# A two-layer Perceiver kernel: the separate context row's product made ahead on GpSimd, one addition for each bank of averages, full-width transposes of the last rows

## The chip, the cores and the metric

The kernel runs on one core of a Trainium2 chip. The metric is the device time of one execution, in microseconds, as the median of several runs.

The core's engines work at once, each through its own instructions in order: TensorE (PE, with its weight loads as PEld), VectorE (DVE), ScalarE (ACT), GpSimd (POOL) and SyncE (SP), which here only issues DMA transfers. They wait for each other by semaphores. Matrix products land in PSUM, which has banks of 512 fp32 numbers for each of 128 partitions; everything else lies in SBUF.

## What is computed

There are 16 batches of 64 latent tokens of width 128 (x), and for each batch a context of 1601 rows. Two layers follow each other; each adds to x a cross-attention over the context, a scan (a state-space recurrence) and a feed-forward part (in layer 0 a small attention with a mixture of experts, in layer 1 a linear block with values rounded to a coarse grid). All is fp32. The part that the change touches most is the cross-attention, cut to its core:

```python
xn, ln_lat = layer_norm(x, g1, b1), layer_norm(latents, g2, b2)
q = ln_lat @ Wq
k, v = split(concatenate([xn, ln_lat], axis=1) @ Wkv)      # 1601 + 64 rows, 16 heads of 64
weight = softmax(where(mask, einsum('bhld,bhnd->bhln', q, k) * scale, neg))
out = einsum('bhln,bhnd->bhld', weight, v) @ Wout
```

The scan of layer 0 runs 16 states over 64 tokens: h = exp(A dt) h + dt u B_t, y = sum over the states of h C_t.

## The kernel before

**Attention.** Weights are folded so that queries meet the normalised context rows directly, and averages of context rows are projected afterwards. A *group* is one layer, one batch and half of the heads: 64 groups in order, each with 512 columns (8 heads of 64 queries). A group has 13 steps (NT), one for each 128 keys: rows 0 to 1535 in 12 chunks, and a last chunk of 64 context rows (1536 to 1599) with the 64 latents below them. Row 1600, the *row apart*, does not fit; it is treated by itself.

At each step n the function step() writes, in this order: scores() of the newest group (L706, a 128x512 product into one of three PSUM banks "s"; L714 or L716, the running maximum R on VectorE; L719 or L721, the eviction to st on ScalarE); average() of the group begun LAG = 23 steps earlier (L820, two banks "av", one for each pair of query blocks, with a 129th column that sums the weights); gather() at that group's end; then the steps of self.plan for the group between: partial, joint, handed, everywhere, own_max, apart_weight at fixed step numbers counted from the group's end, which find each column's maximum, and weigh(), which subtracts it (L807) and takes the exponential (L808). fp32 products appear twice in the profile, as two passes.

**The row apart.** For each group apart_weight() makes ee, its weight for each query: df is subtracted on VectorE (L786) from the group's own maxima m4, which came by DMA (L779), and ScalarE takes the exponential (L787). xeb is the normalised row with a 1 behind it, broadcast to all partitions by a DMA 14 steps into the batch (L1595). gather() leaves PSUM and adds the row at once: for each of the two banks, two instructions on VectorE (L829) make aq = xeb * ee + av. Then denominator() takes reciprocals (L868) and scales aq on GpSimd (L869), turn() transposes, and output() projects. The very last group goes through finish() instead.

**Context.** In layer 0, context() normalises a batch's rows (L666, L675), writes them to DRAM for layer 1, transposes them four chunks at a time on TensorE (L685) and evicts the result twice on ScalarE (L688, for layer 0 and for layer 1); the last chunk goes as a 64-row transpose. GpSimd then scales the rows (L624), and a DMA puts the latents into the last chunk's lower half (L626). The first batch takes a path of its own (first_context), with its own 64-row transpose at L574.

**Everything else** lies beside it. The stages scan0 and moe (layer 0, four rounds) and scan1 and ffn (layer 1, five rounds) are generators; run() advances them with a budget for each step, so that they fill the engines beside the attention of later batches. The scan of scan0 has for each state s two exponentials (L977), a product db on GpSimd (L978), the scan itself on VectorE (L989), a product with C (L994) and a sum on GpSimd (L995). B and C rows come broadcast by DMA as bb, two states at a time (L974).

A scheduler orders the instructions of each engine; the contexts behind() keep new work from going further ahead than a given earlier score step on TensorE, VectorE and ScalarE. Buffers are rotating tiles: a tile of the same tag waits until the earlier one's readers are done.

Of the kernel before, what the change touches and what calls it, by code (L numbers as in the profile page):

```python
# [32 lines left out]
F32 = mybir.dt.float32  # L33
# [4 lines left out]
ALU = mybir.AluOpType  # L38
# [4 lines left out]
P = 128  # L43
NB, L, D = 16, 64, 128
# [3 lines left out]
G = 12  # L48
REM = 64
# [18 lines left out]
NS = 16  # L68
# [10 lines left out]
TG = CG * P  # L79
# [4 lines left out]
class Kernel:  # L84
# [543 lines left out]
    def context(self, lay, b):  # L628

        nc = self.nc  # L630
        w1, b1 = self.vecs_of(lay)[:2]
        kv, kvT = self.kv_of[lay, b]
        n = G + 1
        if (lay, b) == (0, 1):

            mv = self.sm([P, n, 2], "fmv", bufs=2)
            rstd, off = (self.sm([P, n], f"c{x}") for x in ("rstd", "off"))
            for k in range(n):
                bs = self.sm([P, 6], "fbs")
                nc.vector.bn_stats(bs, kv[:, k, :D])  # L640
                nc.vector.bn_aggr(mv[:, k, :], bs)
                if k % 2:
                    yield 1.0
            nc.vector.tensor_scalar_add(rstd, mv[:, :, 1], EPS)
            self.rsqrt(rstd, rstd, n)
            nc.gpsimd.tensor_tensor(off, mv[:, :, 0], rstd, ALU.mult)
            nc.gpsimd.tensor_scalar(off, off, -1.0, None, ALU.mult)
            for k in range(8, n):
                nc.gpsimd.tensor_scalar(kv[:, k, :D], kv[:, k, :D], mv[:, k, 0:1], rstd[:, k:k + 1], ALU.subtract, ALU.mult)
            yield HOP3  # L650
            for k in range(8):
                nc.scalar.activation(kv[:, k, :D], kv[:, k, :D], AF.Identity, scale=rstd[:, k:k + 1], bias=off[:, k:k + 1])
                if k % 2:
                    yield 1.0
        elif lay == 0:
            nc.gpsimd.memset(kv[64:P, G, :D], 0.0)
            nmean, rstd, v, off = (self.sm([P, n], f"c{x}") for x in ("mean", "rstd", "var", "off"))
            for lo, hi in ((0, 7), (7, n)):
                nc.vector.tensor_reduce(nmean[:, lo:hi], kv[:, lo:hi, :D], AX.X, ALU.add)
                if lo == 0:  # L660
                    yield 1.0
            nc.vector.tensor_scalar_mul(nmean, nmean, -1.0 / D)
            yield 0.2
            for k in range(n):
                scr = self.at.tile([P, D], F32, tag="cscr", name=f"scr{b}_{k}", bufs=1)
                nc.scalar.activation(scr, kv[:, k, :D], AF.Square, bias=nmean[:, k:k + 1], accum_out=v[:, k:k + 1])  # L666
                if k in (3, 6, 9):
                    yield 0.0
            yield HOP1
            nc.vector.tensor_scalar(v, v, 1.0 / D, 1e-5, ALU.mult, ALU.add)  # L670
            self.rsqrt(rstd, v, n)
            nc.gpsimd.tensor_tensor(off, nmean, rstd, ALU.mult)  # L672
            yield HOP5
            for k in range(n):
                nc.scalar.activation(kv[:, k, :D], kv[:, k, :D], AF.Identity, scale=rstd[:, k:k + 1], bias=off[:, k:k + 1])  # L675
                if k in (3, 6, 9):
                    yield 0.0
        if lay == 0:
            nc.sync.dma_start(out=self.xh[b], in_=kv[:, :, :D])
            yield HOP  # L680
            for g in range(G // 4 + 1):
                w, m = (512, P) if g < G // 4 else (REM, REM)
                t = self.tp(f"kt{b}_{g}")
                for k in range(4 * g, min(4 * g + 4, n)):
                    nc.tensor.transpose(t[:, (k - 4 * g) * P:(k - 4 * g) * P + m], kv[:m, k, :D], self.ident[:m, :m])  # L685
                raw = self.at.tile([P, 512], F32, tag="kts", name=f"kts{b}_{g}", bufs=1)
                for to, by in ((kvT[:, g * 512:g * 512 + w], w1), (raw[:, :w], YG1)):
                    nc.scalar.activation(to, t[:, :w], AF.Copy, scale=self.vcol[:, by:by + 1])  # L688
                nc.sync.dma_start(out=self.xhT[b][:, g * 512:g * 512 + w], in_=raw[:, :w])
                yield HOP3  # L690
        yield from self.with_latents(lay, b)
# [89 lines left out]
    def apart_weight(self, g):  # L781
# [5 lines left out]
        nc.scalar.activation(ee, df, AF.Exp)  # L787
        grp["ee"] = ee

    def spread(self, v, name):  # L790

        t = self.tp(name)
        for k in range(4):
            self.nc.tensor.transpose(t[:, k * P:(k + 1) * P], v[:, k:k + 1].to_broadcast([P, P]), self.ident)  # L794
        return t
# [26 lines left out]
    def gather(self, g, j):  # L822

        nc, grp = self.nc, self.groups[g]
        if j == 0:
            grp["aq"] = self.at.tile([P, 4, D + 1], F32, tag="aq", name=f"aq{g}", bufs=2)
        xeb, av = self.xeb_of[grp["key"][:2]], grp.pop(("av", j))
        for k in range(2):
            nc.vector.scalar_tensor_tensor(grp["aq"][:, 2 * j + k, :], xeb, grp["ee"][:, 2 * j + k:2 * j + k + 1], av[:, k, :], ALU.mult, ALU.add)  # L829
        if j:  # L830
            for k in ("st", "R", "mb"):
                grp.pop(k)
# [66 lines left out]
    def scan0(self, gr):  # L899
        nc, tc, a = self.nc, self.tc, self.a  # L900
        X = self.X[:, gr * CG:(gr + 1) * CG, :]
        with tc.tile_pool(name="sc1", bufs=1) as one, ExitStack() as later:
            t1 = lambda shape, name: one.tile(shape, F32, tag=name, name=f"sc_{name}")
# [4 lines left out]
            two = lambda name: a[name].rearrange("(k p) n -> p k n", p=P)  # L908
# [16 lines left out]
            both = [P, 2, TG]  # L925
# [7 lines left out]
            g = self.tp("g")  # L933
            for k in range(2):
                nc.tensor.matmul(g[:, k * TG:(k + 1) * TG], W_gate[:, k * P:(k + 1) * P], xT, start=True, stop=True)
            th = t1(both, "y")
# [11 lines left out]
            t = self.tp("bc")  # L948
# [3 lines left out]
            bcd = self.dram.tile([2, NS, TG], F32, tag=f"bcd{gr}", name=f"bcd{gr}")  # L952
            nc.sync.dma_start(out=bcd.rearrange("j s t -> (j s) t"), in_=bcT)
            first.close()
            work = later.enter_context(tc.tile_pool(name="sc2", bufs=2))
# [5 lines left out]
            u = t1(both, "u")  # L961
# [4 lines left out]
            y = t1(both, "y")  # L966
            yield 1.2

            def ahead(s):
                nonlocal bb  # L970
                if s % 2 == 0:
                    bb = work.tile([P, 2, 2, TG], F32, tag="bb", name=f"bb{s}")
                    for j in range(2):
                        nc.sync.dma_start(out=bb[:, j], in_=bcd[j, s:s + 2, :].partition_broadcast(P))  # L974
                da, db = (work.tile(both, F32, tag=n, name=f"{n}{s}") for n in ("da", "db"))
                for k in range(2):
                    nc.scalar.activation(da[:, k, :], dt[:, k, :], AF.Exp, scale=na[:, k, s:s + 1])  # L977
                nc.gpsimd.tensor_tensor(db, u, self.row(bb[:, 0, s % 2, :], both), ALU.mult)  # L978
                return da, db, self.row(bb[:, 1, s % 2, :], both)

            bb = None
            made = ahead(0)
            yield HOP
            for s in range(NS):
                da, db, cc = made
# [237 lines left out]
    def scan1(self, c0, CG):  # L1223
        nc, tc, a = self.nc, self.tc, self.a
        X = self.X[:, c0:c0 + CG, :]
        TG, BG = CG * P, 2 * CG
        NH, HD = 4, 64
        last = c0 + CG == C and CG == 1
        with tc.tile_pool(name="sd1", bufs=1) as one, tc.tile_pool(name="sd2", bufs=CG) as work:
            t1 = lambda shape, name: one.tile(shape, F32, tag=name, name="sd_" + name)  # L1230
            ld = lambda name, shape, src=None: self.load(name, shape, a[name] if src is None else src, one)
            two = lambda name: a[name].rearrange("(k p) n -> p k n", p=P)
# [19 lines left out]
            xc, th = t1([P, 2, TG], "xc"), t1([P, 2, TG], "th")  # L1252
# [11 lines left out]
            else:  # L1264
                t = self.tp("xz")
# [19 lines left out]
            t = self.tp("sdt")  # L1285
# [3 lines left out]
            shape = [P, CG, NH]  # L1289
            dt, adt = t1(shape, "dt"), t1(shape, "adt")  # L1290
            e, w, v, ln = (t1(shape, n) for n in ("spe", "spw", "spv", "spl"))
# [7 lines left out]
            t = self.tp("sz")  # L1299
# [23 lines left out]
                        nc.tensor.matmul(t[:, hh * TG:(hh + 1) * TG], m[:, k, hh * P:(hh + 1) * P], xc[:, k, :], start=(k == 0), stop=(k == 1))  # L1323
                nc.scalar.copy(dst.rearrange("p h t -> p (h t)"), t[:, :2 * TG])

            bT, cT = t1([P, 2, TG], "bT"), t1([P, 2, TG], "cT")
            bc(bT, BwT)
            yield 0.4
            yield HOP1
# [5 lines left out]
            both = [slice(b * L, (b + 1) * L) for b in range(2)]  # L1335
            af = [work.tile(full, F32, tag="af", name=f"af{c}") for c in range(CG)]
            for c in range(CG):
                x = nc.vector.tensor_tensor(af[c], self.row(self.after, full), self.bc(adt[:, c, :], full), ALU.mult)
# [6 lines left out]
            t = self.tp("sx")  # L1345
# [13 lines left out]
            for c in range(CG):  # L1359
                gs = [self.tp(f"gr{c}{i}") for i in range(2)]  # L1360
                for k in range(2):
                    for i in range(2):
                        part = slice(i * HD, (i + 1) * HD)
# [16 lines left out]
            for dst, i in ((zb, 2), (z, 0)):  # L1380
                for k in range(2):
                    x = nc.scalar.activation(dst[:, k, :], z[:, k, :], AF.Copy, scale=self.ycol[:, i + k:i + k + 1])
# [19 lines left out]
            t = self.tp("syt")  # L1402
# [6 lines left out]
            t = t[:, :2 * TG]  # L1409
# [118 lines left out]
    def run(self, out):  # L1528
# [2 lines left out]
        self.groups = [{"key": (lay, b, half)} for lay in range(2) for b in range(NB) for half in range(2)]  # L1531
        ng = len(self.groups)
        self.plan = (
            ((0, self.partial), (2, self.joint), (3, self.handed), (5, self.everywhere), (7, self.own_max), (11, self.apart_weight)),
            ((1, self.maximum), (3, self.spread_max)),
        )
        per_layer = NB * 2 * NT
# [1 line left out]
        done = lambda lay, b: start(lay, b) + LAG + 10  # L1539
# [44 lines left out]
        while n < (ng + 1) * NT + LAG + 8 or between:  # L1584
            for lay in range(2):
                for b in range(NB):
# [6 lines left out]
                    if n == start(lay, b) + 14:  # L1593
                        xeb = self.xeb_of[lay, b] = self.at.tile([P, D + 1], F32, tag="xeb", name=f"xeb{lay}_{b}", bufs=2)
                        self.nc.sync.dma_start(out=xeb, in_=self.xed[lay][b].partition_broadcast(P))  # L1595
            while prep and prep[0][0] <= n:
                key, _, g = prep.pop(0)
# [191 lines left out]
```

## Time and profile before

| what | value |
|---|---|
| time, median of 3 runs | 1936.54 us (1932.92 to 1939.88) |
| the profiled execution's own time | 1938.11 us |
| its span, first to last instruction | 1936.4 us, TensorE's granted clock 0.996 |
| TensorE matmul busy | 1883.0 us, 97% (11738 instructions) |
| VectorE busy | 1633.4 us, 84% (3186) |
| ScalarE busy | 1357.9 us, 70% (2635) |
| GpSimd busy | 511.8 us, 26% (584) |
| score matmuls L706 | 862.8 us, 1664 passes |
| average matmuls L820 | 884.6 us, 6656 passes |
| gather L829 on VectorE | 76.7 us, 252 instructions |
| scaling L869 on GpSimd | 71.7 us, 63 instructions |
| DMA | 112.64 MB, mean 58 GB/s |

A row of the profile names line, engine and operation, output and inputs with their shapes, then the count; behind the bar stand the busy time and the mean length of one, and then the time that the engine sat idle just before and what ended that idle time. Shares of busy time are averages over stages that have different limits; a matmul's end is modelled, so that consecutive passes overlap in the rows. A wait row says who waited, for which line on which engine, the sum in us, the number of times and the longest.

### The profile page before, as it was taken

The numbers are of one execution on the slowest core, as the hardware profiler recorded it, in microseconds if no ns is written. First come the engines' busy times: TensorE is split into PE (matmuls) and PEld (weight loads), VectorE is DVE, ScalarE is ACT, GpSimd is POOL, SyncE is SP. The second block draws the span as 40 slices with busy tenths as digits, with TensorE's granted clock in tenths as the row PEclk, the third lists the DMA queues.
The fourth block names the chain that finished last, engine by engine and source line by source line (L and its number), as shares of the span: only waits on it lengthen the run. The fifth ranks groups of instructions, "written<-read, shape, count | busy, mean of one in ns | idle before, by whom it ended". The sixth has DMA issues, their size and how long they took to land. (4 is left out here: it accounts for less than half of the span.)

```text
span 1936.4 us, 32717 instructions
## 1 busy us (share of the span) xinstructions
PE 1883.0 (97%) x11738; PEld 1426.3 (74%) x11738; DVE 1633.4 (84%) x3186; ACT 1357.9 (70%) x2635; POOL 511.8 (26%) x584
## 2 busy tenths in 40 slices
PE   9999999998999999999999999999999999999998
PEld 5777777676777767777667787767778777776786
DVE  7987777998878998886998978999787998877984
ACT  5888887897869888776665757767566565765651
POOL 5122122543214453121443203453101121102000
PEclk9999999999999999999999999999999999999999
DMA  6121112321123131232232102222120211201100
GB/s 194 36 58 55 55 55 77 86 64 45 54 82 94 57 82 49 69 95 68 73 79 59 40 25 75 71 71 55 42 58 21 60 38 38 59 2 38 25 2 23
DMA packets 192268, 112.64 MB, mean 58 GB/s; under 512 B 56030, under 2 KB 174570, under 8 KB 192106
## 3 DMA queue, kind: packets, MB, share of 16 engines
q1 hardware_dynamic: 187278, 109.77, 20.6%
q8 instruction: 93, 1.52, 0.3%
q10 hardware_dynamic: 4828, 0.78, 0.2%
q14 instruction: 69, 0.57, 0.1%
HBM read 81.41 MB, written 27.54 MB: 56 GB/s over the span
## 5 line engine op out<-in xcount | busy, mean ns | idle before, releaser
L820 PEld LDWEIGHTS av<-kv,st 128*128 128x128 f32 x6656 | 870.2, 192 | 365.6 <-issue 346.3
L820 PE MATMUL av<-kv,st 128*128 128x129 f32 x6656 | 884.6, 276 | 2.2 <-DVE aq L829 2.1
L706 PE MATMUL s<-qT,kvT 128*128 128x512 f32 x1664 | 862.8, 601 | 15.7 <-ACT st L721 10.5
L808 ACT ACTIVATE st<-st 128x1024 f32<-128x1024 f32 (+1 forms) x448 | 444.4, 997 | 130.2 <-DVE st L807 124.2
L807 DVE TENSOR_TENSOR st<-st,mb 128x1024 f32<-128x1024 f32 (+1 forms) x448 | 504.2, 1130 | 2.0 <-PE mb L794 1.5
L719 ACT ACTIVATE st<-s,mcol 128x512 f32<-128x512 f32 x416 | 282.7, 683 | 219.4 <-DVE R L714 197.5
L721 ACT COPY st<-s 128x512 f32<-128x512 f32 x416 | 239.9, 582 | 108.1 <-DVE R L716 100.2
L714 DVE SCALAR_TENSOR_TENSOR R<-s,mcol,R 128x512 f32<-128x512 f32 x352 | 261.5, 743 | 57.2 <-PE s L706 55.2
L716 DVE TENSOR_TENSOR R<-s,R 128x512 f32<-128x512 f32 x352 | 240.2, 682 | 67.0 <-PE s L706 65.2
L706 PEld LDWEIGHTS s<-qT,kvT 128*128 128x128 f32 x1664 | 254.8, 192 | 35.9 <-ACT st L721 18.4
L624 POOL TENSOR_TENSOR kv<-kv,vec 128x384 f32<-128x384 f32 (+1 forms) x128 | 133.7, 1059 | 242.6 <-PE kt L685 68.9
L869 POOL TENSOR_TENSOR aq<-aq,rd 128x512 f32<-128x512 f32 x63 | 71.7, 1138 | 254.4 <-DVE rd L868 241.7
L978 POOL TENSOR_TENSOR db<-sc_u,bb 128x512 f32<-128x512 f32 x64 | 84.9, 1329 | 120.1 <-DVE h L989 61.2
L995 POOL TENSOR_TENSOR sc_y<-sc_y,h 128x512 f32<-128x512 f32 x60 | 79.6, 1327 | 117.6 <-DVE h L994 116.9
L989 DVE TENSOR_TENSOR_SCAN h<-da,db 128x512 f32<-128x512 f32 x64 | 85.7, 1339 | 0.0
L675 ACT ACTIVATE kv<-kv,coff,crstd 128x128 f32<-128x128 f32 x182 | 77.9, 494 | 8.5 <-POOL coff L672 8.5
L829 DVE SCALAR_TENSOR_TENSOR aq<-xeb,ee,av 128x129 f32<-128x129 f32 x252 | 76.7, 339 | 0.6 <-issue 0.4
L666 ACT ACTIVATE scr<-kv,cmean 128x128 f32<-128x128 f32 x182 | 72.3, 397 | 0.8
L498 PE MATMUL q<-xnT,wqk 128*128 128x128 f32 x512 | 68.4, 277 | 2.7 <-ACT qT L507 2.3
L498 PEld LDWEIGHTS q<-xnT,wqk 128*128 128x128 f32 x512 | 63.0, 192 | 7.7 <-ACT qT L507 2.5
L139 POOL TENSOR_TENSOR crstd<-cvar,neghalf 128x13 f32<-128x13 f32 x14 | 34.8, 2487 | 120.5 <-DVE cvar L670 98.9
L892 PEld LDWEIGHTS o<-wvo,aT 128*128 128x128 f32 x512 | 59.4, 192 | 5.3 <-issue 3.6
(425 smaller groups left out, 1821.4 us busy)
## 6 DMA issues: line engine op xcount, KB each, us to landing
bb<-bcd SPq DMA_DIRECT2D x64, 256.0 KB
xh<-kv SPq DMA_DIRECT2D x16, 832.0 KB
kv<-xh SPq DMA_DIRECT2D x16, 832.0 KB
kvT<-xhT SPq DMA_DIRECT2D x16, 800.0 KB
kv<-in_ctx_dram SPq DMA_DIRECT2D x15, 768.0 KB
xhT<-kts SPq DMA_DIRECT2D x45, 256.0 KB
ew<-in_e1T_dram SPq DMA_DIRECT2D x36, 64.0 KB
ew<-in_e3T_dram SPq DMA_DIRECT2D x36, 64.0 KB
```

What stands on the lines that cost most here:

```text
L498: nc.tensor.matmul(t[:, k * P:(k + 1) * P], self.wqk[:, g * 4 + k, :], xnT, start=True, stop=True)
L624: nc.gpsimd.tensor_tensor(kv[:, lo:hi, :D], kv[:, lo:hi, :D], self.row(self.vec[:, w1, :], [P, hi - lo, D]), ALU.mult)
L706: mm = nc.tensor.matmul(s, self.kv_of[lay, b][1][:, i * P:(i + 1) * P], q, start=True, stop=True)
L714: mx = nc.vector.scalar_tensor_tensor(R, s, mc, last, ALU.add, ALU.max)
L716: mx = nc.vector.tensor_tensor(R, s, last, ALU.max)
L719: ev = nc.scalar.activation(st, s, AF.Identity, bias=mc)
L721: ev = nc.scalar.copy(st, s)
L807: nc.vector.tensor_tensor(st, st, self.row(mb, [P, n, NQ]), ALU.subtract)
L808: nc.scalar.activation(st, st, AF.Exp)
L820: nc.tensor.matmul(grp["av", j][:, k, :], st, self.kv_of[lay, b][0][:, i, :], start=(i == 0 and k == 0), stop=(i == NT - 1 and k == 1))
L978: nc.gpsimd.tensor_tensor(db, u, self.row(bb[:, 0, s % 2, :], both), ALU.mult)
L989: nc.vector.tensor_tensor_scan(flat(h), flat(da), flat(db), 0.0, ALU.mult, ALU.add)
```

## The change

There are four edits.

1. A new step of the plan, apart_part(), stands two steps behind apart_weight(). It makes the product of the row apart and its weights for all four query blocks of a group in one instruction on GpSimd (128x516, both operands broadcast) into a new tile with one buffer. In gather(), one addition of 128x258 for each bank takes the place of the two instructions with a multiply and an add.
2. In context(), the transpose of the last chunk takes all 128 rows and gives 128 columns; the evictions still read the first 64.
3. In scan0, the broadcast rows bb come one state at a time, B and C together, into three buffers of half the size; the next state's transfer is issued together with the work ahead of the present one.
4. In scan1, cT takes the buffer that th had (tag "th", which yT takes after it).

finish(), and the first batch's context, are unchanged.

```diff
--- before.py
+++ after.py
@@ -679,10 +679,10 @@
             nc.sync.dma_start(out=self.xh[b], in_=kv[:, :, :D])
             yield HOP
             for g in range(G // 4 + 1):
-                w, m = (512, P) if g < G // 4 else (REM, REM)
+                w = 512 if g < G // 4 else REM
                 t = self.tp(f"kt{b}_{g}")
                 for k in range(4 * g, min(4 * g + 4, n)):
-                    nc.tensor.transpose(t[:, (k - 4 * g) * P:(k - 4 * g) * P + m], kv[:m, k, :D], self.ident[:m, :m])
+                    nc.tensor.transpose(t[:, (k - 4 * g) * P:(k - 4 * g + 1) * P], kv[:, k, :D], self.ident)
                 raw = self.at.tile([P, 512], F32, tag="kts", name=f"kts{b}_{g}", bufs=1)
                 for to, by in ((kvT[:, g * 512:g * 512 + w], w1), (raw[:, :w], YG1)):
                     nc.scalar.activation(to, t[:, :w], AF.Copy, scale=self.vcol[:, by:by + 1])
@@ -787,6 +787,12 @@
         nc.scalar.activation(ee, df, AF.Exp)
         grp["ee"] = ee
 
+    def apart_part(self, g):
+
+        grp, shape = self.groups[g], [P, 4, D + 1]
+        part = grp["apart"] = self.at.tile(shape, F32, tag="apart", name=f"apart{g}", bufs=1)
+        self.nc.gpsimd.tensor_tensor(part, self.row(self.xeb_of[grp["key"][:2]], shape), self.bc(grp["ee"], shape), ALU.mult)
+
     def spread(self, v, name):
 
         t = self.tp(name)
@@ -824,9 +830,8 @@
         nc, grp = self.nc, self.groups[g]
         if j == 0:
             grp["aq"] = self.at.tile([P, 4, D + 1], F32, tag="aq", name=f"aq{g}", bufs=2)
-        xeb, av = self.xeb_of[grp["key"][:2]], grp.pop(("av", j))
-        for k in range(2):
-            nc.vector.scalar_tensor_tensor(grp["aq"][:, 2 * j + k, :], xeb, grp["ee"][:, 2 * j + k:2 * j + k + 1], av[:, k, :], ALU.mult, ALU.add)
+        two = slice(2 * j, 2 * j + 2)
+        nc.vector.tensor_tensor(grp["aq"][:, two, :], grp["apart"][:, two, :], grp.pop(("av", j)), ALU.add)
         if j:
             for k in ("st", "R", "mb"):
                 grp.pop(k)
@@ -966,19 +971,23 @@
             y = t1(both, "y")
             yield 1.2
 
+            def fetch(s):
+                x = fetched[s] = work.tile([P, 2, TG], F32, tag="bb", name=f"bb{s}", bufs=3)
+                nc.sync.dma_start(out=x, in_=bcd[:, s, :].partition_broadcast(P))
+
             def ahead(s):
-                nonlocal bb
-                if s % 2 == 0:
-                    bb = work.tile([P, 2, 2, TG], F32, tag="bb", name=f"bb{s}")
-                    for j in range(2):
-                        nc.sync.dma_start(out=bb[:, j], in_=bcd[j, s:s + 2, :].partition_broadcast(P))
+                for x in range(s, min(s + 2, NS)):
+                    if x not in fetched and x not in done:
+                        fetch(x)
+                bb = fetched.pop(s)
+                done.add(s)
                 da, db = (work.tile(both, F32, tag=n, name=f"{n}{s}") for n in ("da", "db"))
                 for k in range(2):
                     nc.scalar.activation(da[:, k, :], dt[:, k, :], AF.Exp, scale=na[:, k, s:s + 1])
-                nc.gpsimd.tensor_tensor(db, u, self.row(bb[:, 0, s % 2, :], both), ALU.mult)
-                return da, db, self.row(bb[:, 1, s % 2, :], both)
-
-            bb = None
+                nc.gpsimd.tensor_tensor(db, u, self.row(bb[:, 0], both), ALU.mult)
+                return da, db, self.row(bb[:, 1], both)
+
+            fetched, done = {}, set()
             made = ahead(0)
             yield HOP
             for s in range(NS):
@@ -1323,7 +1332,7 @@
                         nc.tensor.matmul(t[:, hh * TG:(hh + 1) * TG], m[:, k, hh * P:(hh + 1) * P], xc[:, k, :], start=(k == 0), stop=(k == 1))
                 nc.scalar.copy(dst.rearrange("p h t -> p (h t)"), t[:, :2 * TG])
 
-            bT, cT = t1([P, 2, TG], "bT"), t1([P, 2, TG], "cT")
+            bT, cT = t1([P, 2, TG], "bT"), one.tile([P, 2, TG], F32, tag="th", name="sd_cT")
             bc(bT, BwT)
             yield 0.4
             yield HOP1
@@ -1531,7 +1540,7 @@
         self.groups = [{"key": (lay, b, half)} for lay in range(2) for b in range(NB) for half in range(2)]
         ng = len(self.groups)
         self.plan = (
-            ((0, self.partial), (2, self.joint), (3, self.handed), (5, self.everywhere), (7, self.own_max), (11, self.apart_weight)),
+            ((0, self.partial), (2, self.joint), (3, self.handed), (5, self.everywhere), (7, self.own_max), (11, self.apart_weight), (13, self.apart_part)),
             ((1, self.maximum), (3, self.spread_max)),
         )
         per_layer = NB * 2 * NT
```

## The prediction

> **What bounds the kernel now.** I read the busy times first, then a table of windows, the waits of TensorE and ScalarE, the timeline, and last single lines of the code. The head of the page, of the execution before:
>
> ```profile
> PE 1883.0 (97%) x11738; PEld 1426.3 (74%) x11738; DVE 1633.4 (84%) x3186; ACT 1357.9 (70%) x2635; POOL 511.8 (26%) x584
> ```
>
> TensorE is idle for only 1936.4 - 1883.0 = 53.4 us of the span. Five of these lie in the first 60 us, 8.2 in the last 48 (from 1888 us on). About 40 us in the middle are all that a lighter VectorE can give back. Where they lie is seen in windows (columns: stretch, its length, then busy time and count of PE, PEld, DVE, ACT and POOL, clock, DMA):
>
> ```profile
> 315.00:420.00 105.00, 100.58 (x597) 74.44 (x596) 102.46 (x166) 91.50 (x208) 55.29 (x48) 1.00 0.28 76
> 612.00:752.00 140.00, 134.06 (x805) 100.45 (x804) 133.42 (x206) 119.10 (x268) 67.53 (x59) 1.00 0.28 75
> 916.00:1023.00 107.00, 101.60 (x609) 74.98 (x608) 103.33 (x161) 72.51 (x120) 46.40 (x39) 0.98 0.27 73
> 1180.00:1336.00 156.00, 151.51 (x887) 111.67 (x885) 150.78 (x240) 112.36 (x179) 67.39 (x59) 1.00 0.24 62
> ```
>
> In these 508 us VectorE is 95 to 98% busy and TensorE idles 4.4 + 5.9 + 5.4 + 4.5 = 20.3 us. In the other 1320 us of the middle VectorE is 81% busy, and TensorE idles 20 us. The stretches are those of scan0 over batches that still have their attention to do. What TensorE waits for, between 60 and 1888 us, and what ScalarE waits for:
>
> ```profile
> PE s L706 <- ACT st L721: 9.5, 13, 1.7
> PE s L706 <- ACT st L719: 4.6, 8, 1.1
> PE tm L758 <- DVE four L751: 3.6, 6, 1.3
> ...
> PE av L820 <- DVE aq L829: 2.1, 3, 1.2
> ```
> ```profile
> ACT st L719 <- DVE R L714: 197.5, 202, 5.5
> ```
>
> The score matmul waits for ScalarE to empty a score bank, and ScalarE in turn for VectorE's running maximum R. So a late VectorE shows as "ACT st". The chain of waits is VectorE queue, eviction, bank, TensorE.
>
> **The change part by part.** The sum is made against the profiled execution, 1938.1 us (span 1936.4 and 1.7 around it). The median of the three runs, 1936.5, is 1.6 lower, and I take that off at the end. About 0.3%, 5.8 us, is what a measurement of this kernel can tell from no change.
>
> *Transposes (L685).* The 64-row transpose of the last context rows becomes a 128-row one, 15 times. TensorE's timeline around one of them (start, length, line):
>
> ```profile
> 330.53 1.05 PE L820 MATMUL av<-kv,st 128*128 128x129 f32 x8
> 331.52 0.27 PE L685 MATMUL kt<-ident,kv 64*128 64x64 f32 x1
> 331.72 1.12 PE L706 MATMUL s<-qT,kvT 128*128 128x512 f32 x2
> ```
>
> Eight av passes in 1.05 us with the last 0.28 long start every 0.11 us, so the eighth starts at 331.30. The small transpose starts 0.22 us after it, the next matmul 0.20 us after that, where full-size passes follow each other by 0.11. The small shape costs 0.09 + 0.09, about 0.19 us. All fifteen look the same, and one stands before a 1.5 us stall, so 14 x 0.19 = 2.7 us come off TensorE's own work, with no cover needed. Lower bound 0, if the gaps are the place's and not the shape's.
>
> *VectorE.* For each of 126 banks (63 groups by two) two instructions at L829 become one addition of 128x258. The DVE timeline, and the nearest row for the new form:
>
> ```profile
> 353.04 0.59 DVE L829 SCALAR_TENSOR_TENSOR aq<-xeb,ee,av 128x129 f32<-128x129 f32 x2
> 353.55 0.68 DVE L716 TENSOR_TENSOR R<-s,R 128x512 f32<-128x512 f32 x1
> 354.15 0.59 DVE L829 SCALAR_TENSOR_TENSOR aq<-xeb,ee,av 128x129 f32<-128x129 f32 x2
> 354.67 1.21 DVE L807 TENSOR_TENSOR st<-st,mb 128x1024 f32<-128x1024 f32 x1
> ```
> ```profile
> L1397 DVE TENSOR_TENSOR sd_y<-sd_y,sy x8: 404/415/422, 1487.9 to 1914.4; 128x256 f32<-128x256 f32 x8
> ```
>
> A pair takes 0.51 us from its start to the next start, 0.08 less than it lasts, because ends overlap. L1397, also an addition of one PSUM and one SBUF operand of nearly this size, lasts 0.415, so about 0.33. Saved: 0.18 to 0.19 a bank, x126 = 24 us. With no overlap for the new form it is 0.10 a bank, 13 us; at L716's rate (0.60 us for 512 columns, so 0.30) 27. I take 24, since L1397 is nearest.
>
> *GpSimd.* It gets 63 products of 128x516 (apart_part). The nearest row is L869, 128x512 with one broadcast operand, 1.14 us on average; L624, with the other operand broadcast, has 1.29. So 63 x 1.14 = 72 us (65 at L869's 1.03 minimum, 81 by L624). POOL goes from 26 to 30%. The product stands right behind the weights ee (step 13, ee at step 11), mostly after L869 and before L624 or db in GpSimd's order. In the trace the first L829 of a group starts 12 us at the least and 23 us in the middle after its ee. That lead hides the product. Were it gone, the gather would wait on VectorE with R (L714, L716) and the weights (L807) queued behind it, score banks would stay full, and TensorE would stop for about the missing time, 1.1 us a group. With one buffer, the product also waits for the additions of the group before; they end 1.3 us or more before the new ee, so I give it nothing.
>
> *GpSimd in VectorE's way.* The medians and maxima of three lines with two SBUF operands (min/median/max in ns):
>
> ```profile
> L751 DVE TENSOR_TENSOR four<-part,sx x63: 199/226/1289, 38.1 to 1841.0; 128x64 f32<-128x64 f32 x63
> L989 DVE TENSOR_TENSOR_SCAN h<-da,db x64: 1181/1215/2222, 330.9 to 1319.0; 128x512 f32<-128x512 f32 x64
> L994 DVE TENSOR_TENSOR h<-h,bb x60: 642/680/1590, 341.9 to 1323.8; 128x512 f32<-128x512 f32 x60
> ```
>
> Their means are 436, 1339 and 799 ns. Mean less median, times count, is 13.2 + 7.9 + 7.1 = 28 us, lost where GpSimd ran beside them. Lines with a PSUM operand (L716, L807) show no such tail. GpSimd's 72 us more are 14% of its 512: by share 4 us. Laying 1.14 us behind each ee of the trace (and behind what GpSimd then does), 17 of 63 products would hold up such an instruction, 11 us in all. I take 8; the ends are 0 and rival B. Net relief of VectorE: 24 - 8 = 16 us.
>
> The Trainium skill ("SBUF — State Buffer", "Who interferes with whom") speaks against this part: two SBUF operands on VectorE and a reading GpSimd instruction exclude each other for a whole instruction. The tails above agree in kind; by that rule, with every product in VectorE's way for half its length, the cost would be an estimated 36 us and the part would lose 12.
>
> *What reaches TensorE.* Of the 126 banks 38 lie in the four stretches (76 L829 instructions in the windows), 30%: 4.8 us, counted in full, since 20.3 us of stall stand there. The rest, 11.2 us, falls where VectorE mostly has slack; I count a fifth, 2.2. The ends are nothing and, with all 16 us counted in full, 16.
>
> *The rest.* The bb transfers stay 64 of 256 KB each, but one state at a time with three buffers, on SP's queue. SP waits there now for L994, and GpSimd's db waits 33.2 us for bb in all. But the scan L989 shows 0.0 us of idle before it: nothing, and at most a few of the 33 us either way. If SP held longer, the reads of m4 (L779) and context loads stand behind it. cT in th's place waits for L1282, whose result cT is made from, and yT for matmuls long past: nothing. The instruction order shifts on every engine: plus or minus 3 us.
>
> Sum: 2.7 + 4.8 + 2.2 = 9.7 us. 1938.1 - 9.7 = 1928.4, less 1.6: **1927 us**.
>
> **The rivals.** A: VectorE's relief is eaten by the cover. The 40 us of idle are spikes of other work (the mixture stage's hand-overs, L1122, L181), a spared 0.19 us does not reach them, and only the transposes count: 1938.1 - 2.7 - 1.6 = 1934. For it: TensorE is 97% busy. Against it: half of the idle lies where VectorE is full.
>
> B, slower: the product holds VectorE up. It breaks even at 24/63 = 0.38 us for each product. At 0.75 us (L751's worst is 1.06 above its median) VectorE loses 23 us net. 30% of that, 6.9, counts in full, of the remaining 16 a half, since the slack is then smaller: 8. 15 - 2.7 = 12 us more, 1948 to 1950. For it: four (L751) starts a median 3.5 us after ee, and L869 and L624 now push the product toward it. Against it: undisturbed products end before that, and the lines that fill VectorE read PSUM.
>
> C: the product isn't made ahead, because GpSimd's queue is late, and the gather waits. It takes a backlog over 12 us; where all 63 waited 0.3 us, it would cancel the relief: 1936.
>
> **How the numbers follow.** My forecast 0.55, A 0.2, B 0.2, C 0.05. The forecast's own range is 1919 (16 us counted in full) to 1932. B reaches from 1940 up; the range takes in A, C and the lower half of B: 1916 to 1944. Faster by over 0.3% (below 1930.7) takes most of the forecast's case, 0.52. Within 0.3%: its upper end, A, C and a little of B, 0.28. Slower: 0.20.
>
> **What would show it.** Right: DVE busy falls by about 16 us, one addition of some 0.42 us at the gather with no idle before it, POOL up 70 us, TensorE's idle down to some 46 us and its busy time down 3 us, and the small transposes gone. Wrong: means of L751, L989 or L994 well above 436, 1339 and 799 ns (B); a wait of the gather for POOL (C); the same stalls in the four stretches with a lighter VectorE (A).

## The result, and the profile after

The changed kernel takes 1942.5 us (median of 19 runs, 1937.7 to 1945.4), the kernel before beside it 1934.1 (19 runs, 1931.3 to 1939.9). The ratio is **1.0038**, 95% interval 1.0029 to 1.0047: slower by 0.4%, where 0.5% faster was forecast. The profiled execution has a span of 1942.0 us. The head of its page:

```profile
PE 1884.5 (97%) x11738; PEld 1427.3 (73%) x11738; DVE 1624.6 (84%) x3060; ACT 1360.0 (70%) x2635; POOL 584.3 (30%) x647
```

TensorE's idle time is 57.5 us, not the 46 of the forecast. GpSimd gained its 72 us, VectorE lost only 8.8 us of busy time, not 16. The groups that the forecast priced (line, engine, operation, shapes, count, busy us and mean ns, idle before it):

```profile
L998 DVE TENSOR_TENSOR_SCAN h<-da,db 128x512 f32<-128x512 f32 x64 | 90.9, 1421 | 0.0
...
L794 POOL TENSOR_TENSOR apart<-xeb,ee 128x516 f32<-128x516 f32 x63 | 71.5, 1136 | 8.7 <-ACT ee L787 8.5
...
L834 DVE TENSOR_TENSOR aq<-apart,av 128x258 f32<-128x258 f32 x126 | 52.0, 413 | 1.7 <-PE av L826 1.7
L1003 DVE TENSOR_TENSOR h<-h,bb 128x512 f32<-128x512 f32 x60 | 48.4, 807 | 0.0
...
L751 DVE TENSOR_TENSOR four<-part,sx 128x64 f32<-128x64 f32 x63 | 28.8, 457 | 0.6
```

The product and the addition have the predicted lengths (1.14 and 0.42 us), and the addition never waits for GpSimd. The three lines with two SBUF operands are longer than before (1339, 799, 436 ns). TensorE's waits between 60 and 1888 us, and the four stretches of before (columns as there):

```profile
PE s L706 <- ACT st L721: 13.5, 20, 3.3
PE tm L758 <- DVE four L751: 5.1, 6, 1.9
PE s L706 <- ACT st L719: 4.0, 9, 1.1
...
PE av L826 <- DVE aq L834: 1.0, 1, 1.0
```
```profile
315.00:420.00 105.00, 100.57 (x592) 74.00 (x591) 102.21 (x156) 90.40 (x205) 59.74 (x51) 1.00 0.34 76
612.00:752.00 140.00, 132.52 (x784) 98.61 (x783) 132.41 (x189) 115.25 (x255) 70.32 (x63) 0.99 0.32 75
916.00:1023.00 107.00, 98.58 (x580) 71.86 (x579) 101.60 (x149) 69.96 (x111) 53.70 (x42) 0.98 0.35 73
1180.00:1336.00 156.00, 150.97 (x876) 111.02 (x877) 144.99 (x222) 113.34 (x182) 70.58 (x61) 1.00 0.25 60
```

The gather's wait halved, but the waits for an emptied score bank (14.1 us before, 17.5 now) and for four grew. In the stretches TensorE idles 4.4 + 7.5 + 8.4 + 5.0 = 25.4 us, 5 more than before. One wait, of GpSimd for the B and C rows, tripled. Before, and now:

```profile
POOL db L978 <- DMA bb<-bcd: 33.2, 14, 3.6
```
```profile
POOL db L987 <- DMA bb<-bcd: 99.5, 33, 5.0
```

### The profile page after: what moved, and what is told of

Its sections match the earlier page's. It is cut to its first block, busy times and chain, and to the rows that moved or that the text cites. A ratio compares the mean times of both kernels' runs of the same rounds, so it can differ in the third digit from the quotient of the medians.

```text
span 1942.0 us, 32699 instructions
## 1 busy us (share of the span) xinstructions
PE 1884.5 (97%) x11738; PEld 1427.3 (73%) x11738; DVE 1624.6 (84%) x3060; ACT 1360.0 (70%) x2635; POOL 584.3 (30%) x647
## 4 chain that ended last, share of the span: by engine, by line
PE 50%; DVE 14%; issue 4%; ACT 2%; POOL 1%; DMA 1%; POOLq 0%; ACTq 0%; DVEq 0%
PE av L826 19%; PE s L706 18%; DVE st L813 3%; DVE R L714 3%; PE q L498 2%; PE o L897 2%; DVE h L998 1%; DVE R L716 1%; PE at L885 1%; PE me L1131 1%; ACT st L814 1%; PE gu L1145 1%; PE gu L1146 1%; PE sb L1332 1%; DVE h L1003 1%
## 5 line engine op out<-in xcount | busy, mean ns | idle before, releaser
L1004 POOL TENSOR_TENSOR sc_y<-sc_y,h 128x512 f32<-128x512 f32 x60 | 84.3, 1406 | 70.6 <-DVE h L1003 69.9
L998 DVE TENSOR_TENSOR_SCAN h<-da,db 128x512 f32<-128x512 f32 x64 | 90.9, 1421 | 0.0
L794 POOL TENSOR_TENSOR apart<-xeb,ee 128x516 f32<-128x516 f32 x63 | 71.5, 1136 | 8.7 <-ACT ee L787 8.5
```

The costliest lines, as they stand in the source:

```text
L998: nc.vector.tensor_tensor_scan(flat(h), flat(da), flat(db), 0.0, ALU.mult, ALU.add)
```

## The experiments

Ratios are to runs of the kernel before on the same chip, with 95% intervals. The runs come from five series, in which the kernel before has medians of 1933.7 to 1937.5 us; a difference between ratios of two series is uncertain by some 0.15 to 0.2%. One number is a count of mine from the traces: *VectorE's lost time*. For each kind of instruction (operation, tiles and shape) it takes the lower quartile of its length in the kernel before, and sums what every instruction lasts beyond that, where this is over 0.1 us. Before has 48.8 us of it, the changed kernel 60.5.

**The edits one by one.** Edits 2 (t_only) and 3 (b_only) are those hunks of the diff alone. Edit 1 alone has no room for its new tile, so the product goes into aq itself (inplace); abc has edits 1, 3 and 4.

```diff
# inplace: apart_part() and gather()
+        part = grp["aq"] = self.at.tile(shape, F32, tag="aq", name=f"aq{g}", bufs=2)
+        self.nc.gpsimd.tensor_tensor(part, self.row(xeb...), self.bc(grp["ee"], shape), ALU.mult)
...
+        mine = grp["aq"][:, 2 * j:2 * j + 2, :]
+        nc.vector.tensor_tensor(mine, mine, grp.pop(("av", j)), ALU.add)
```

> The kernel before with edit 2 alone: the last context rows turned 128 at a time. By the prediction's step 2.7 us faster, the gaps around the transposes of 0.20 us gone; all theories of the slowdown leave that alone. If the gaps belong to the place and not to the shape: no difference.

> The kernel before with edit 3 alone: bb comes one state at a time into three buffers. No instruction of TensorE, VectorE or ScalarE changes its place. Theory BB (the smaller transfers land later, GpSimd's db waits for them, and the scan of layer 0 holds VectorE up): 5 to 8 us slower than before, GpSimd's wait for bb near 100 us instead of 33, PE's idle up by as much. Theory PORT (the product on GpSimd holds VectorE up) and theory ORDER (the new order of instructions on the engines costs): no difference, within 2 us of before.

> The kernel before with edit 1 alone, made to fit without edits 3 and 4: GpSimd writes the product of the row apart and its weights straight into aq, and the addition at the gather works in place there, so no further tile is needed. Theory BB: the relief of VectorE is free of its price, 3 to 8 us faster than before. Theory PORT: 5 to 8 us slower than before, the means of L751, L989 and L994 clearly above 436, 1339 and 799 ns. Theory ORDER: slower too, by 5 to 8 us, but with those means unchanged.

> The changed kernel without edit 2 (the old 64-row transposes). If edit 2 is worth 2.7 us, 10 to 11 us slower than before, that is 2 to 3 us slower than the change as it stands; if edit 2 itself costs (by the shifted order), nearer to before than the change is. Theories BB and PORT: 9 to 11 us slower than before.

Measured: edit 2 **0.9985** (0.9975 to 0.9994), 3 us as forecast. Edit 3 **1.0022** (1.0012 to 1.0031): it costs 4 us where the forecast had nothing. Edit 1 in aq **0.9983** (0.9972 to 0.9994). Edits 1, 3 and 4 together **1.0048** (1.0033 to 1.0062), where the product of the single ratios is 1.0005: the parts don't add up. In b_only the traces have the instructions of TensorE, VectorE and ScalarE in the order of before, so its loss is late data and not a new order there:

```profile
POOL db L982 <- DMA bb<-bcd: 101.6, 32, 4.6
```

The timeline of VectorE and GpSimd shows what a late bb does (start, length, line). Before:

```profile
393.91 1.27 POOL L978 TENSOR_TENSOR db<-sc_u,bb 128x512 f32<-128x512 f32 x1 [3.44 <-DVE h L989]
```
```profile
394.60 0.67 DVE L716 TENSOR_TENSOR R<-s,R 128x512 f32<-128x512 f32 x1
395.20 0.15 DVE L662 TENSOR_SCALAR cmean<-cmean 128x13 f32<-128x13 f32 x1
395.27 1.21 DVE L807 TENSOR_TENSOR st<-st,mb 128x1024 f32<-128x1024 f32 x1
```

With edit 3 alone, at the same place in the work:

```profile
395.31 1.27 POOL L982 TENSOR_TENSOR db<-sc_u,bb 128x512 f32<-128x512 f32 x1 [4.57 <-DMA bb<-bcd]
```
```profile
394.88 0.67 DVE L716 TENSOR_TENSOR R<-s,R 128x512 f32<-128x512 f32 x1
395.48 1.13 DVE L662 TENSOR_SCALAR cmean<-cmean 128x13 f32<-128x13 f32 x1
396.53 1.20 DVE L807 TENSOR_TENSOR st<-st,mb 128x1024 f32<-128x1024 f32 x1
```

db waits for its transfer, starts 1.4 us later, and now runs beside L662, a tiny instruction that goes from 0.15 to 1.13 us: it ends with db. L807 and all behind it are a microsecond later. No wait of VectorE is seen anywhere in this, only a longer instruction. It is one example: over the whole trace VectorE's lost time is only 0.5 us above that of before (49.3 and 48.8), and by which way the rest of the 4 us goes is not shown.

**How bb comes late.** Before, there are two buffers of two states each. The rows of an even state wait for the reader three states back; an odd state finds its rows in the same buffer, with one state more of lead. All 14 waits of db before are at even states. With the change each transfer is sent one state ahead and waits for the reader three states back, at every state: of the 33 waits 16 are at even and 17 at odd ones. The transfers themselves are not smaller, 64 of 256 KB in both kernels; only the buffer is. b4a sends the same transfers two states ahead into four buffers, which need no more room than before. inplace_b is edit 1 in aq with edit 3, without the tile and cT's move; inplace_t edits 1 and 2; bct edits 2, 3 and 4.

```diff
# b4a, against edit 3
-                x = fetched[s] = work.tile([P, 2, TG], F32, tag="bb", name=f"bb{s}", bufs=3)
+                x = fetched[s] = work.tile([P, 2, TG], F32, tag="bb", name=f"bb{s}", bufs=4)
-                for x in range(s, min(s + 2, NS)):
+                for x in range(s, min(s + 3, NS)):
```

> Edit 3 alone, but with four buffers and two states fetched ahead, as much room as before. Theory DEPTH (edit 3 costs because every state, and no longer every second one, waits for its own transfer a step after its buffer comes free): no slower than before, GpSimd's wait for bb back to 33 us or less. Theory PIECES (the transfers are in pieces of half the size and take longer): still about 4 us slower than before, the wait for bb well above 33 us.

> Edit 1 with the product written into aq, and edit 3. Alone they gave 3.3 us less and 4.2 us more, and the change without edit 2 is 9 us slower than before, so the parts do not add up. Theory MEET (late bb transfers and the new product meet in GpSimd's queue and on VectorE's way, so that together they cost more than apart): 7 to 9 us slower than before. Theory TILE (the separate tile apart, with one buffer, or cT in th's place costs): about 1 us slower than before, the plain sum.

> Edit 1 with the product written into aq, and edit 2, without edits 3 and 4. If the two gains add up: 6 us faster than before (ratio 0.997). If they share the same stalls: 3 to 4 us faster.

> The change without edit 1: edits 2, 3 and 4, the gather as before. Plain sum of the single runs: 1 us slower than before (within 0.1%). The changed kernel is 7.3 us slower than before, so edit 1 in its company would then cost 6 us, where by itself it gains 3: theory MEET. If this run is already 5 us or more slower, edits 2 and 3 disturb each other without edit 1, and MEET falls.

Measured: b4a **0.9994** (0.9985 to 1.0003). The wait of db is gone, and one of the sum is left:

```profile
POOL sc_y L999 <- DMA bb<-bcd: 1.3, 1, 1.3
```

So one state for each transfer costs nothing; its lateness costs 0.28%, b_only against b4a, which have the same order on TensorE, VectorE and ScalarE, and VectorE's lost time differs by 4.0 us (49.3 and 45.3). inplace_b **1.0041** (1.0029 to 1.0053), like abc: the separate tile and cT's place are not needed for the loss. inplace_t **0.9994** (0.9985 to 1.0004), less than either of its edits gains alone. bct **0.9999** (0.9989 to 1.0009): adding edit 1 to it makes the change, and costs 0.39%.

**Is the late bb all of it?** Edit 1 and edit 3 in four buffers (inplace_b4a), the same with edit 2 (inplace_b4a_t), that without edit 1 (t_b4a), and edit 1 with the product made twice (inplace_2x):

```diff
# inplace_2x, apart_part()
         self.nc.gpsimd.tensor_tensor(part, ...)
+        self.nc.gpsimd.tensor_tensor(part, ...)
```

> Edit 1 with the product written into aq itself, and edit 3 with four buffers of bb and the transfer sent two states ahead. Theory LATE BB (edits 1 and 3 cost together because db waits for bb, and GpSimd's work, now with 63 products in it, is thrown later and into VectorE's): the wait of db for bb is gone (under 5 us instead of 96), the sum of VectorE's lost time falls from 54 to 50 us or less, and the ratio is 0.997 to 0.999, as for edit 1 alone with two states a transfer. Rival ORDER (any edit beside edit 1 changes the order of VectorE's and ScalarE's instructions, and this order is a worse one): the wait is gone and the ratio stays at 1.003 to 1.005. Rival PIECES (64 transfers of half the size beside the other DMAs): also 1.003 to 1.005, with other DMA waits longer.

> The kernel before it with edit 2 added: the whole change but cT's buffer, with the product written into aq and bb fetched two states ahead into four buffers. If the parts add up, 0.9983 (edit 1) x 0.9985 (edit 2) x 0.9994 (edit 3 with four buffers) = 0.996, 1929 us. If the gains of edits 1 and 2 overlap, as they did together without edit 3 (0.9994), 0.998 to 1.000. By ORDER 1.002 to 1.004.

> Edit 2 and edit 3 with four buffers and two states ahead, without edit 1. If the parts add up, 0.9985 x 0.9994 = 0.998, 1932 us; TensorE busy 3 to 6 us less than before, no wait of db for bb. If it is 1.000 as with three buffers (edits 2, 3 and 4 together gave 0.9999), the late bb did not cost what it seems to have cost.

> Edit 1 with the product written into aq, and the product made twice, the second time over the first: it doubles GpSimd's part and leaves all else. It measures what a product costs VectorE. GpSimd is busy some 70 us more than with one product (578). The prediction's price, 8 us of VectorE for 63 products of which 30% counts: the time of VectorE lost in its two-SBUF-operand lines up by 6 to 8 us, and 2 to 3 us more than with one product: ratio 0.999 to 1.000. Rival B's price (0.75 us a product, 47 us of VectorE): 1.005 or more. By nothing at all: 0.998.

Measured: **1.0006** (0.9996 to 1.0016), **0.9994** (0.9983 to 1.0005), **0.9958** (0.9943 to 0.9974) and **1.0044** (1.0029 to 1.0059). In time, bb saves 0.35% beside edit 1 (1.0041 to 1.0006), with the same order on TensorE, VectorE and ScalarE in inplace, inplace_b and inplace_b4a; so that order and one state for each transfer don't hold most of the loss of that pair. 0.23% beside edit 1 alone is left, unexplained. And edit 1 still doesn't pay: without it the best kernel stands at 0.9958, with it at 0.9994. And a second product costs 0.61%, 12 us. The price of the product was now the suspect.

**The two halves of edit 1.** relief has only the lighter gather, prod only the product, each on the kernel before and on t_b4a.

```diff
# relief: gather()                      (ee left out of the sum)
+        nc.vector.tensor_tensor(grp["aq"][:, 2 * j:2 * j + 2, :], self.row(xeb, [P, 2, D + 1]), av, ALU.add)
# prod: apart_part() as in inplace, and the old gather() writes over it
```

> Only the gather of edit 1, on the kernel before: one addition of 128x258 for each bank, which adds the row apart itself; its weights ee are left out of the sum (they are still made), and there is no product on GpSimd. It measures what VectorE's relief alone is worth. The prediction's step (24 us off VectorE, 30% of it in full, a fifth of the rest): VectorE busy 24 us less, ratio 0.993 to 0.996. Rival A (the relief reaches nothing): VectorE busy 24 us less, ratio 0.999 to 1.001. Rival ORDER (whatever moves the instructions costs): 1.001 to 1.003.

> Only the product of edit 1, on the kernel before: GpSimd makes it into aq, and the old gather, two instructions a bank, writes over it. It measures what the product alone costs. The prediction's price (8 us of VectorE, a third of it on the path): 1.001 to 1.002. Theory PRODUCT (as doubling it showed, 1.0044 against 0.9983): 1.004 to 1.006, VectorE's lost time up by 6 to 10 us. Nothing: 0.999 to 1.000.

> The same relief (the weights left out of the sum, no product) on the kernel with edit 2 and with edit 3 in four buffers, whose ratio is 0.9958. If the relief is worth what the prediction says, 0.989 to 0.992; if it reaches nothing, 0.995 to 0.997; if any new order costs, 0.998 or more. Together with the product alone it must give the 0.9994 that both together had on this kernel.

> The product alone (made into aq, written over by the old gather) on the kernel with edit 2 and with edit 3 in four buffers, whose ratio is 0.9958. The prediction's price: 0.997 to 0.998. Theory PRODUCT: 1.000 to 1.002. Nothing: 0.995 to 0.996.

Measured: relief alone **0.9944** (0.9931 to 0.9956), 10.8 us. Product alone **1.0036** (1.0024 to 1.0049), 7.0 us. Their product is 0.9980; both together had 0.9983. The page and the gather of relief:

```profile
PE 1879.2 (98%) x11738; PEld 1424.3 (74%) x11738; DVE 1605.5 (84%) x3060; ACT 1360.2 (71%) x2635; POOL 511.7 (27%) x584
```
```profile
L828 DVE TENSOR_TENSOR aq<-xeb,av 128x258 f32<-128x258 f32 x126 | 51.8, 411 | 1.5 <-PE av L820 1.5
```

VectorE is 27.9 us lighter and TensorE's idle time falls from 53.4 to 42.2. On t_b4a, from 0.9958: relief 0.9949 (0.9936 to 0.9961), worth 0.1% there by the ratios, where the prediction's rule gave 0.4 to 0.7%; product 1.0023 (1.0012 to 1.0034), which costs 0.65%. The pages of t_b4a and of t_b4a with the product:

```profile
PE 1876.3 (97%) x11738; PEld 1424.4 (74%) x11738; DVE 1625.3 (84%) x3186; ACT 1357.2 (70%) x2635; POOL 509.9 (26%) x584
```
```profile
PE 1881.8 (97%) x11738; PEld 1426.9 (74%) x11738; DVE 1633.3 (84%) x3186; ACT 1356.6 (70%) x2635; POOL 576.2 (30%) x647
```

The VectorE instructions are the same, and take 8.0 us more beside the product (lost time 40.8 and 49.2 us). TensorE idles 55.9 us in place of 50.8, and its busy time is up by 5.5. Here, as in the other pairs with and without the product (before and prod, relief and inplace, relief_t_b4a and inplace_b4a_t, inplace and inplace_2x), the traces have the instructions of TensorE, VectorE and ScalarE in the same order; so the product's price is no matter of their order.

**Does it have to be GpSimd?** act_b and act_t_b4a make the product on ScalarE, on the same two kernels.

```diff
# act_b, apart_part()
-        self.nc.gpsimd.tensor_tensor(part, ...)
+        for k in range(4):
+            self.nc.scalar.activation(part[:, k, :], xeb, AF.Copy, scale=grp["ee"][:, k:k + 1])
```

> Edit 1 on the kernel before, with the product written into aq and made on ScalarE, by four instructions of 128x129 a group, in place of the one on GpSimd: GpSimd gets nothing more. By the last group's own row (L850, 128x128 with a weight for each partition, 0.39 us) it adds 252 x 0.39 = 99 us to ScalarE's 1358. Theory BESIDE (the product costs because it runs on GpSimd beside VectorE): VectorE's lost time stays at 41 to 46 us, and the ratio lies below the 0.9983 that the product on GpSimd had, 0.995 to 0.997, less what ScalarE's evictions lose. Rival ANYWHERE (whatever engine makes it, another 70 to 100 us of work in the shadow of this schedule cost TensorE some 7 us): 0.998 to 1.001. Rival SCALAR (ScalarE, which empties the score banks, becomes late): above 1.002, with TensorE's wait for the eviction of st up from 14 to 25 us or more.

> The same product on ScalarE, on the kernel with edit 2 and with edit 3 in four buffers (0.9958 without edit 1, 0.9994 with the product on GpSimd, 0.9949 with the relief alone). BESIDE: 0.995 to 0.996. ANYWHERE: 0.998 to 1.000. SCALAR: above 1.001.

```profile
L795 ACT ACTIVATE aq<-xeb,ee 128x129 f32<-128x129 f32 x252 | 81.7, 398 | 0.0
```

Measured: **0.9977** (0.9968 to 0.9986) and **0.9984** (0.9976 to 0.9993), beside 0.9983 and 0.9994 with GpSimd. VectorE's lost time falls to 45.9 us from 54.7, as BESIDE had it, but at most 0.1% of time comes of it, within the intervals. SCALAR falls: TensorE's waits for the eviction are 15.9 us in act_b, 14.1 before. 0.9984 is a number of ANYWHERE; 0.9977 lies between it and BESIDE, nearer to ANYWHERE. On either engine the product eats most of what the relief brings, or more than all of it where edits 2 and 3 stand beside it.

## Why the prediction was wrong

*Transposes: right.* 2.7 us forecast, 0.15% measured, and all 195 passes of L685 are now 128x128.

*VectorE's relief: right.* By the prediction's own rule 24 us of it bring 24 x 0.30 in full and a fifth of the rest, 7.2 + 3.4 = 10.6 us. Relief alone measured 10.8, with an interval of 8.5 to 13.3; so near a hit is luck, the more as VectorE became lighter by 27.9. The place fits too: between the same score passes, the four stretches of the profiled execution are 7.1 us shorter than before (15.0 over the whole span). Rival A, that the relief reaches nothing, falls on this kernel.

*The product's price: the first step that failed.* Its length (72 us, measured 71.5), the hidden lead and, on average, the lost time of VectorE were sized well: the five pairs with and without a product differ by 2.2 (before), 8.4 (t_b4a), 14.2 (relief), 13.3 (relief on t_b4a) and, for the second product, 9.9 us, 9.6 in the mean, where 8 was forecast. What failed was netting those 8 us against the 24 and passing on less than half of the remainder. This prices the product at 3.5 us of time; measured are, in the same order, 7.0, 12.6, 7.5, 8.7 and 12 us, 9.5 in the mean. So on average the price is as large as VectorE's lost time. Pair by pair the two don't follow each other, and how a product delays TensorE stays open; a part in some pairs is TensorE's clock (last section). Rival B had the right sign and a total (12 us more, measured 8) nearer to the result, but by luck: its 0.75 us a product would be 47 us of VectorE, the measured loss is 0.03 to 0.23 us a product, and late bb had no part in it. ScalarE pays about the same, 0.33 and 0.35%, with 5.4 and 5.2 us of VectorE's lost time; but there the order on the engines changes too, so it doesn't tell the way.

The Trainium skill ("SBUF — State Buffer", "Who interferes with whom") agrees in kind: L662, held until db ends, is a block for a whole instruction. The estimate of 36 us that the prediction worked out from it was nearly four times the measured 9.6 us (mean of the five pairs), so most of the products' time was not in VectorE's way.

*The rest, bb priced at nothing: the second step that failed.* The prediction saw db's 33.2 us of waiting and discarded it, because the scan L989 shows 0.0 us of idle before it. That was the wrong witness. VectorE works in order and is 95 to 98% busy there, with other work in front of the scan; a late db can shift GpSimd's work into other instructions instead, as at L662. Late bb costs 0.28% on the kernel before, 0.35% beside edit 1 and 0.41% beside edit 2 (bct to t_b4a, edit 4 aside): 5 to 8 us. The count that would have told: three buffers of one state give every state the lead that before only the even ones had, and before it was the even ones that waited.

*The sum.* The gains were added as if independent. Even the plain product of the single runs of edits 1, 2 and 3 is 0.9990; the change has 1.0038. Relief is worth 10.8 us on the kernel before and 1.7 on t_b4a by the ratios (5.7 by the times, which come from two series). Firmer is what one series shows: with the relief, the kernel ends at 1923.2 us without edit 2 and edit 3 in four buffers, and at 1923.3 with them. The gains overlap, as if they removed the same stalls; which stalls was not traced. Costs don't overlap like that: edit 1 nets -0.17% on the kernel before, +0.09% beside edit 2, +0.12% beside edit 3 in four buffers, +0.36% beside both. Thus the change in steps, each measured: edit 2 and edit 3 in four buffers 0.9958; with edit 1, 0.9994; with one state's lead, three buffers, the separate tile and cT moved, 1.0038. No single repair makes the forecast true: with bb in time the change is no faster than before.

*Rival C* did not happen: the additions waited 1.7 us in all, for TensorE. *Order:* plus or minus 3 us was allowed for it. b_only needs none of it, and edit 1's new order on TensorE, VectorE and ScalarE stands in relief as well, which is faster by 10.8 us. *Two slips* of the working change nothing: 0.22 us is 0.11 and not 0.09 above 0.11, so a small transpose costs 0.20 us; and with all 16 us in full its sum is 1918, not 1919.

**The faster version** is t_b4a, 128-row transposes and bb two states ahead in four buffers with the old gather: 1928.9 us beside 1937.0, 0.9958 (0.9943 to 0.9974).

## What to carry to other kernels

An operation moved to an idle engine is not free because that engine is idle: price what it delays on the critical engine where that is full, separately from what it relieves, and don't net the two before asking how much reaches the end. When a buffer is cut into smaller ones, count the lead that each transfer then has, in steps of the consumer, and keep it by more buffers; a consumer without idle time before it is no proof that late data cost nothing. Measure two gains together before adding them.

## What the runs showed of the hardware

TensorE's clock falls to half for 3.41 us after some short stalls, which adds up to 1.7 us to each. In the profiled execution of the kernel before this happens four times ahead of the end, after stalls of 1.44, 2.25, 2.87 and 2.62 us; after one of 3.04 us it doesn't. One of them (timeline of TensorE):

```profile
1002.75 1.07 PE L344 MATMUL WvT<-rawWo,rawWvT 64*128 64x128 f32 x4 [2.25 <-DVE X L896]
...
1004.34 1.91 PE L706 MATMUL s<-qT,kvT 128*128 128x512 f32 x2
...
1007.10 1.02 PE L706 MATMUL s<-qT,kvT 128*128 128x512 f32 x2
```

The pair of score passes after a 2.25 us stall takes 1.91 us; the next takes 1.02. The Trainium skill ("TensorE: Matmul & The Clock Gate", "What's actually happening") gives 3.4 us as the idle time that halves the clock, in windows that run free of the program; here 2.25 us were enough, and the measurement decides. The free-running window agrees with the trace: the four falls start 709.97, 395.95 and 361.81 us after one another, 208, 116 and 106 times 3.413 us. Executions of one kernel differ by it: in 115 runs of the kernel before, those with a mean clock of 0.998 or more have a median of 1932.4 us (11 runs), those with 0.994 or less 1939.0 (29 runs). A stall near 2 us that an edit adds or removes can so count nearly twice.

How much of the results that is can be estimated. Over the 115 runs, 0.001 of the mean clock goes with 1.5 us. The runs of the product alone have a mean clock of 0.9946, those before beside them 0.9969: some 3.4 of its 7.0 us. With the second product it is 0.9950, with one 0.9975: 3.7 of 12 us. The runs of edit 1 in aq have 0.9975, those before 0.9952: 3.4 us, as much as all that edit 1 gains alone. In the pairs with relief it is no part of the price: inplace stands 0.0023 above its runs of before, relief 0.0015 above its own.
